# First attention of an eight-layer model: TensorE's order in a quartet written as a table of single steps

## The chip, the core and the metric

The kernel runs on one core of one Trainium2 chip. Its time is the device time of one execution in microseconds (us); the median of three runs before the change is 2110.02 (2104.93 to 2113.53). Everything is float32. A core has five engines that work side by side and wait for one another through semaphores: TensorE (PE in the profile; PEld is its weight load), VectorE (DVE), ScalarE (ACT), GpSimd (POOL) and SyncE (SP), which issues DMAs. Matmul results land in PSUM, which the kernel treats as eight banks of 128 x 512 numbers.

## The reference

The input x has shape (2, 512, 512): two batches (b) of 512 tokens with 512 features. Four attentions and four feed-forward layers follow, each of the form x = x + f(layernorm(x)). Only the first attention is changed:

```python
C_q  = x @ Wq_d  + bq_d                      # 512 -> 12
C_kv = x @ Wkv_d + bkv_d                     # 512 -> 4, keys and values share it
q = (C_q @ W_qk + b_qk).reshape(b, s, 32, 4)
scores = einsum('bqhd,bkd->bhqk', q, C_kv) / sqrt(4)
attn = softmax(scores)                       # no mask
V = (C_kv @ Wv_u + bv_u).reshape(b, s, 32, 16)
out = einsum('bhqk,bkhd->bqhd', attn, V).reshape(b, s, 512)
return out @ Wo + bo
```

There are 32 heads in each batch, with a contraction of only four numbers in the scores. The layer after it is a linear map with a low-rank adapter.

## The kernel before

`attn_latent_small` (from L416) does the first attention. A **quartet** is four heads of one batch: there are 16 quartets, 0 to 7 for batch 0 and 8 to 15 for batch 1. Head g of a quartet lies on partitions 32g to 32g+31 (`rows[g]`), so its matmuls use one of four row groups of the array, and four matmuls of different g can run at the same time. Each matmul is recorded as two passes of TensorE.

One quartet u consists of these steps, as functions:

- `score(u, qt, g)` (L560): for one head and one tile of 128 queries, TensorE computes the scores (L563) into a bank, and VectorE takes the row maximum (L571) into `nm[u % 2]`. There are 16 per quartet.
- `maxima(u)` (L575): four transposes of `nm` (L579), and VectorE adds the negated maxima to the queries, giving `qm` (L581).
- `transposed(u, kc, g)` (L584): TensorE computes the scores again with keys on the partitions and the maximum already subtracted (L598), and ScalarE takes the exponent into SBUF (L601). There are 16 per quartet.
- `values(u)` (L603): 16 matmuls that contract over all 128 partitions, four of them accumulating side by side into one bank (L609). ScalarE copies the result (L619) for the first quartet of a half batch, VectorE adds it to `raw` for the others (L621).

Every step takes its PSUM bank from `k.turn()`, which hands out the eight banks strictly in order, so a step can only begin once the step eight before it has been read out of its bank by VectorE or ScalarE.

After quartets 3, 7, 11 and 15 `divide` transposes `raw` and divides by the sums (L631, L636, L639). After quartets 7 and 15 `flatten` (POOL, L652) and `project` (L662, L664, L667) finish a batch and add it to x. `norms` starts the loads of the adapter layer (class `AdaptedBlock`, L729) after quartet 7, and normalises the tokens of batch 0 for it.

Some work runs between the quartets as **extra pieces**: for batch 1, four layernorms (transposes at L195), the latents and queries (chains of four matmuls, L162), two groups of head queries (L478) and the transposed values (L492); and, for the projection, `fold` and `fold_bias` (L501 to L525), which multiply Wv_u into Wo. There are eleven. `fold_bias` also adds a bias to all eight tiles of x on POOL.

`run_quartets` sets TensorE's order; the other engines' order is left to the scheduler, apart from `issue_after`. It first issues all 16 scores of quartet 0 and its maxima. Then, for each u, it alternates four scores of quartet u+1 with four exponents of quartet u, four times over; after each such round comes one extra piece, if any is left, or one of `after` (divide, flatten, project, norms) of an earlier quartet. Then come values(u) and maxima(u+1). In the last quartet the pieces of `ending` (the adapter's weights, its first products, the end of the attention) stand between the exponents. `run_ordered`, which the last attention uses, is another such function, with an order given as a string.

Of the kernel before, what the change touches and what calls it, by code (L numbers as in the profile page):

```python
# [37 lines left out]
B, S, D = 2, 512, 512  # L38
P = 128
NT = S // P  # L40
# [5 lines left out]
class Block:  # L46
# [292 lines left out]
                )  # L339

    @staticmethod
    def run_quartets(n, score, maxima, transposed, values, after, extra, ending):

        due, extra = [], list(extra)
        for u in range(-1, n - 1):
            pieces = [due.pop(0)] if due else []  # L350
            for j in range(NT):
                for m, (kind, g) in enumerate(
                    ((0, 0), (1, 1), (0, 2), (1, 3), (0, 1), (1, 0), (0, 3), (1, 2))
                    if j
                    else ((0, 0), (0, 1), (0, 2), (0, 3), (1, 0), (1, 1), (1, 2), (1, 3))
                ):
                    if kind == 0 and u + 1 < n:
                        score(u + 1, j, g)
                    if kind == 1 and 0 <= u < n:
                        transposed(u, j, g)  # L360
                if extra and u >= 0:
                    extra.pop(0)()
                elif pieces and j < 3:
                    of, done = pieces[0]
                    if done < len(after):
                        after[done](of)
                        pieces[0] = (of, done + 1)
            for of, done in pieces:
                for f in after[done:]:
                    f(of)  # L370
            if 0 <= u < n - 2:
                values(u)
                due.append((u, 0))
            maxima(u + 1)
        for i in range(NT * 4):
            transposed(n - 1, i // 4, i % 4)
            if i == 5:
                values(n - 2)
                for f in after:
                    f(n - 2)  # L380
            if i > 5 and i % 2:
                ending.pop(0)()
        ending.pop(0)()
        values(n - 1)
        for f in ending:
            f()

    @staticmethod
    def run_ordered(n, lead, order, score, maxima, transposed, values, after):

        scores = iter([(u, j, g) for u in range(n) for j in range(NT) for g in (0, 2, 1, 3)])
        for i in range(lead):
            score(*next(scores))
        for u in range(-1, n):
            left = [(j, g) for j in range(NT) for g in (1, 3, 0, 2)] if u >= 0 else []
            for step in order:  # L400
                if step == "S":
                    at = next(scores, None)
                    if at:
                        score(*at)
                elif step == "T" and left:
                    transposed(u, *left.pop(0))
                elif step == "M" and u + 1 < n:
                    maxima(u + 1)
                elif step == "|" and u > 0:
                    after(u - 1)  # L410
            if u >= 0:
                values(u)
        after(n - 1)


def attn_latent_small(k, a):  # L416
# [8 lines left out]
    with ExitStack() as ctx:  # L425
# [19 lines left out]
        for i in range(2):  # L445
            m = one([P, NT, P], f"nm{i}")
# [11 lines left out]
        def prepare(b):  # L458

            xT = k.xT[b]  # L460
            cq = one([P, S], "cq")

            def latents():
                ps = k.turn()
                k.chain(ps, [(wkvd[:, c], xT[:, c]) for c in range(KC)])
                nc.vector.tensor_scalar(keys[b], ps, bkvc, None, ALU.add)

            def queries():
                ps = k.turn()
                k.chain(ps, [(wqd[:, c], xT[:, c]) for c in range(KC)])  # L470
                nc.vector.tensor_scalar(cq, ps, bqd, None, ALU.add)

            def heads(half):
                for g in range(4):
                    t = 4 * half + g
                    own_rows = slice(32 * g, 32 * g + 32)
                    ps = k.turn()
                    nc.tensor.matmul(ps, wqk[own_rows, half], cq[own_rows], start=True, stop=True)  # L478
                    if b == 0 and g % 2:
                        nc.vector.tensor_scalar(  # L480
                            qs[b][:, t], ps, bqk[:, t : t + 1], 0.5, ALU.add, ALU.mult
                        )
                    else:
                        nc.scalar.activation(
                            qs[b][:, t], ps, AF.Identity, bias=halves[:, t : t + 1], scale=0.5
                        )

            def values():

                tp = k.turn()  # L490
                for t in range(NT):
                    nc.tensor.transpose(tp[:, bass.ts(t, P)], keys[b][:, bass.ts(t, P)], k.ident)  # L492
                part = tp.rearrange("p (t d) -> p t d", t=NT)[:, :, 0:5]
                for i in range(4):
                    to = vals[b][:, :, i, 5 * i : 5 * i + 5]
                    k.latest = nc.vector.tensor_copy(to, part).ins

            norms = [lambda t=t: k.layernorm(b * NT + t, k.turn) for t in range(NT)]
            return (norms if b else []) + [latents, queries, lambda: heads(0), lambda: heads(1), values]
# [45 lines left out]
        def behind(piece):  # L545

            def f():
                with tc.issue_after(first):
                    piece()
            return f  # L550

        with tc.issue_after(k.latest):
            adapter_coefficients(k, a)
        extra = [behind(f) for f in prepare(1) + [fold, fold_bias]]

        quartets = [(b, half, i) for b in range(B) for half in range(2) for i in range(4)]
        qm, probs, sums, ctxs = {}, {}, {}, {}
# [2 lines left out]
        def score(u, qt, g):  # L560
            b, half, i = quartets[u]
            ps = k.turn()
            nc.tensor.matmul(  # L563
                ps,
                qs[b][rows[g], 4 * half + i, bass.ts(qt, P)],
                keys[b][rows[g]],
                start=True,
                stop=True,
            )
            at = 32 * g + spare  # L570
            nc.vector.tensor_reduce(  # L571
                nm[u % 2][:, qt, at : at + 1], ps, AX.X, ALU.max, negate=True
            )

        def maxima(u):  # L575
            b, half, i = quartets[u]
            tp = k.turn()
            for qt in range(NT):
                nc.tensor.transpose(tp[:, bass.ts(qt, P)], nm[u % 2][:, qt], k.ident)  # L579
            t = lp.tile([P, S], F32, tag="qm", name="qm")  # L580
            nc.vector.tensor_tensor(t, tp, qs[b][:, 4 * half + i], ALU.add)  # L581
            qm[u] = t
# [20 lines left out]
        def values(u):  # L603
            b, half, i = quartets[u]
            acc = k.turn()
            for kc in range(NT):
                pt = probs.pop((u, kc))
                for g in range(4):
                    nc.tensor.matmul(  # L609
                        acc[rows[g]],  # L610
                        vals[b][:, kc, i],
                        pt[:, g],
                        start=(kc == 0),
                        stop=(kc == NT - 1),
                    )

            if i == 0:
                sums[b, half] = one([P, S], "raw")
                nc.scalar.copy(sums[b, half], acc)  # L619
            else:  # L620
                nc.vector.tensor_tensor(sums[b, half], acc, sums[b, half], ALU.add)  # L621
# [64 lines left out]
        last = len(quartets) - 1  # L686
        adapt = [lambda m=m: blocks[0].adapt(m) for m in range(KC)]
        feed = [lambda t=t: blocks[0].product(0, t) for t in range(NT)]

        tokens = [lambda t=t: k.layernorm(t, k.turn, back=True) for t in range(NT)]  # L690
        ending = [lambda: None] + adapt + feed[:2]
        ending += [lambda: divide(last), feed[2], lambda: flatten(last), feed[3]]
        ending += [lambda: project(last)] + tokens
        after = [divide, flatten, project, norms]
        with tc.manual_schedule(engines={mybir.EngineType.PE}):
            k.run_quartets(
                len(quartets), score, maxima, transposed, values, after, extra, ending
            )
        return blocks[0]


# [1159 lines left out]
```

## Time and profile before

| | us |
|---|---|
| three runs: median (lowest, highest) | 2110.02 (2104.93, 2113.53) |
| the profiled execution | 2103.46 |
| its span, first to last instruction | 2101.4 |
| first score of the first attention (L563) | 23.49 |
| first exponent matmul (L598) | 37.79 |
| maxima of quartets 6 and 7 (L579) | 139.93, 154.00 |
| values of quartets 14 and 15 (L609) | 276.55, 292.24 |
| mean granted clock of TensorE | 0.992 |

The profile is one execution. Times are microseconds from the start of the span. A row of a timeline gives the start, the length, the engine, the line, the operation, the output and the inputs by the program's names (so a bank is called sc, pj, tp or av), the shape and a count; in brackets stands how long the engine was idle before it, and what released it. A row of the table of waits gives the engine and its line, what it waited for, the total, how often and the longest. The stretches give, for each window, the busy time and count of PE, PEld, DVE, ACT and POOL, the granted clock of TensorE and the DMA share and rate.

### The profile page before, as it was taken

Reading aid. Unit: us, or ns where it says so; the run is one execution under the profiler, and the core shown is the slowest. Engines: PE = TensorE matmul, PEld = TensorE weight load, DVE = VectorE, ACT = ScalarE, POOL = GpSimd, SP = SyncE. Lnnn points to the kernel's source line nnn. Section 1 sums busy time; section 2 is a strip of 40 time slices with the busy share of each in tenths; the row PEclk is TensorE's granted clock in tenths of the full one; section 3 lists DMA queues with packets and bytes.
Section 4 is the critical chain, followed back from the end, with each engine's and each line's share of the span. In section 5 each row is a group of like instructions: output and inputs, shape, how many; then the busy total and the mean of one; then the engine's idle time right before and its main releaser. Section 6 shows DMA issues by size and latency. Waiting matters only on the chain. (4 is left out here: it accounts for less than half of the span.)

```text
span 2101.4 us, 40138 instructions
## 1 busy us (share of the span) xinstructions
PE 2031.9 (97%) x15560; PEld 1147.1 (55%) x15560; DVE 1351.0 (64%) x3575; ACT 745.4 (35%) x2072; POOL 970.4 (46%) x1239
## 2 busy tenths in 40 slices
PE   9999999999999999999999989999999999999998
PEld 5444435666666566666665544545454454654654
DVE  7678766756566566666664557666666784855845
ACT  3555632222222222222222145444544411441531
POOL 1101016776555557566653246555555555115220
PEclk9999999999999999999999999999999999999999
DMA  3001012222222222222220321010101003002001
GB/s 100 16 21 41 1 66 76 72 76 71 91 71 71 91 71 76 71 91 76 73 77 26 117 61 54 22 51 25 50 22 52 2 6 70 2 2 41 2 2 40
DMA packets 70221, 107.43 MB, mean 51 GB/s; under 512 B 13699, under 2 KB 50691, under 8 KB 63237
## 3 DMA queue, kind: packets, MB, share of 16 engines
q1 hardware_dynamic: 69380, 103.71, 15.6%
q8 instruction: 126, 2.06, 0.4%
q10 hardware_dynamic: 640, 1.05, 0.3%
q14 instruction: 75, 0.61, 0.1%
HBM read 80.61 MB, written 2.10 MB: 39 GB/s over the span
## 5 line engine op out<-in xcount | busy, mean ns | idle before, releaser
L263 ACT ACTIVATE room<-room,nmax 128x128 f32<-128x128 f32 (+3 forms) x384 | 212.3, 555 | 484.2 <-DVE nmax L253 482.7
L274 POOL TENSOR_SCALAR room<-room,invs 128x128 f32<-128x128 f32 (+3 forms) x384 | 198.0, 537 | 142.1 <-DVE invs L271 142.1
L314 PE MATMUL sc<-turned,vals 32*128 32x128 f32 (+7 forms) x1034 | 186.2, 411 | 1.3 <-DVE turned L287 1.3
L314 PE MATMUL pj<-turned,vals 32*128 32x384 f32 (+7 forms) x708 | 184.9, 422 | 0.0
L210 POOL TENSOR_TENSOR rstd<-ve,mhalf 128x1 f32<-128x1 f32 x80 | 45.9, 577 | 246.0 <-DVE ve L208 240.2
L314 PE MATMUL tp<-turned,vals 32*128 32x256 f32 (+7 forms) x770 | 147.1, 420 | 2.5 <-DMA vals<-v 2.1
L242 PE MATMUL sc<-kT,q 128*32 128x256 f32 (+4 forms) x1528 | 134.0, 384 | 6.8 <-DVE invs L271 4.1
L287 DVE STREAM_TRANSPOSE turned<-room 128x1152 f32<-128x1152 f32 x80 | 109.1, 1363 | 42.4 <-POOL room L274 39.9
L314 PEld LDWEIGHTS sc<-turned,vals 32*128 32x128 f32 (+1 forms) x1034 | 119.3, 166 | 14.3 <-issue 4.2
L943 POOL TENSOR_TENSOR q<-q,cosq 128x512 f32<-128x512 f32 x60 | 89.5, 1491 | 59.9 <-DVE t L940 59.9
L162 PE MATMUL sc<-w,room 128*128 128x512 f32 (+1 forms) x256 | 112.1, 582 | 0.0
L314 PEld LDWEIGHTS pj<-turned,vals 32*128 32x128 f32 (+1 forms) x708 | 104.0, 169 | 4.0 <-issue 1.6
L314 PEld LDWEIGHTS tp<-turned,vals 32*128 32x128 f32 (+1 forms) x770 | 97.6, 169 | 10.8 <-issue 4.9
L162 PE MATMUL sc<-w,ctxT 128*128 128x512 f32 x224 | 101.5, 596 | 0.0
L218 DVE TENSOR_TENSOR x<-sc,x 128x512 f32<-128x512 f32 x79 | 54.2, 686 | 73.0 <-PE sc L162 70.3
L242 PE MATMUL tp<-kT,q 128*32 128x512 f32 (+4 forms) x984 | 91.7, 407 | 4.5 <-DVE invs L271 3.8
L274 POOL TENSOR_SCALAR probs<-probs,invs 128x128 f32<-128x128 f32 (+3 forms) x128 | 65.8, 535 | 65.0 <-DVE invs L271 61.2
L263 ACT ACTIVATE probs<-probs,nmax 128x128 f32<-128x128 f32 (+3 forms) x128 | 71.1, 556 | 65.5 <-DVE nmax L253 64.3
L253 DVE CUSTOM_DVE_ANT_0 room<-sc,mask 128x256 f32<-128x256 f32 (+3 forms) x149 | 70.7, 474 | 35.6 <-PE sc L242 34.1
L242 PE MATMUL pj<-kT,q 128*32 128x288 f32 (+3 forms) x968 | 89.6, 404 | 2.9 <-POOL q L1211 1.9
L944 POOL TENSOR_TENSOR q<-q,t 128x512 f32<-128x512 f32 x64 | 88.0, 1374 | 6.5 <-DVE q L943 2.5
L1208 POOL TENSOR_TENSOR t<-t,sinq 128x512 f32<-128x512 f32 x32 | 40.8, 1276 | 106.4 <-DVE invs L271 100.6
(621 smaller groups left out, 6232.9 us busy)
## 6 DMA issues: line engine op xcount, KB each, us to landing
w<-in_b_wq SPq DMA_DIRECT2D x16, 1024.0 KB, 4.9
w<-in_b_wo SPq DMA_DIRECT2D x16, 1024.0 KB, 5.2
vals<-v SPq DMA_DIRECT2D x256, 64.0 KB, 2.0
w<-in_m_wo SPq DMA_DIRECT2D x8, 1024.0 KB, 7.2
w<-in_b_wk SPq DMA_DIRECT2D x16, 256.0 KB, 2.5
w<-in_b_wupv SPq DMA_DIRECT2D x16, 256.0 KB, 2.5
w<-in_f_w SPq DMA_DIRECT2D x4, 1024.0 KB, 6.0
w<-in_m_wqn SPq DMA_DIRECT2D x8, 384.0 KB, 3.1
```

Of the source, the lines that this page charges most:

```text
L162: last = self.nc.tensor.matmul(out, lhsT, rhs, start=(i == 0), stop=(i == len(pairs) - 1))
L210: self.nc.gpsimd.tensor_tensor(r, ve, self.mhalf, ALU.pow)
L218: self.latest = self.nc.vector.tensor_tensor(self.x[t], ps, self.x[t], ALU.add).ins
L242: nc.tensor.matmul(ps[32 * i : 32 * i + 32, a - lo : b - lo], q[:, at : at + 32], keys[:, a:b], start=True, stop=True,)
L253: nc.vector.tensor_tensor_reduce(out=row, in0=ps[:, :kv], in1=self.mask_back[:, :kv] if qt % 2 else self.mask[:, S - kv :], op0=ALU.add, o ...
L263: nc.scalar.activation(row, row, AF.Exp, bias=nmax, scale=-1.0, accum_out=total[:, qt : qt + 1])
L274: self.nc.gpsimd.tensor_scalar(row, row, inv[:, qt : qt + 1], 1.0, ALU.mult, ALU.mult)
L287: self.nc.vector.transpose(out[:, :last], probs[:, :last])
L314: self.nc.tensor.matmul(out[:, :, :n], values(i, j), rhs, start=(j == blocks[0]), stop=(j == stop[i]),)
L943: mul.tensor_tensor(q, q, tables["cosq"], ALU.mult)
L944: nc.gpsimd.tensor_tensor(q, q, t2, ALU.add)
L1208: nc.gpsimd.tensor_tensor(t2, t2, sinq, ALU.mult)
```

## The change

TensorE's order in the quartets is now a table of single steps, `order`, read by a new function `in_order`. `S10+2` is the score of tile 1 and head 0 for the quartet two ahead, `T32+0` the exponent step of key tile 3 and head 2 of the present quartet, `M` the maxima, `V` the values, and `|` a place for a piece. One reading of the table is one quartet. Twelve of a quartet's 16 scores are issued two or three quartets ahead. The maxima of the next quartet stand among the scores before the values, no longer behind them.

The reading starts three quartets early, so that three, then 12, then 16 scores precede the first exponents. In the last two of these readings an extra piece stands at each of the four bars, and in quartets 0, 1 and 2 one piece each at the second bar. `fold` and `fold_bias` are moved in the list, to stand ahead of and behind the queries. `divide`, `flatten`, `project` and `norms` come at the next bars after their quartet. In quartet 15 the list `ending` has lost its empty first entry, so that two of the adapter's products, and not one, stand ahead of the last values, and the divide follows the values directly.

```diff
+    @staticmethod
+    def in_order(n, order, do):
+        steps = [(s[0], int(s[1]), int(s[2]), int(s[3:])) if s != "|" else s for s in order.split()]
+        for p in range(-3, n + 3):
+            for step in steps:
+                if step == "|":
+                    if p > -3:
+                        do(p, step)
+                elif 0 <= p + step[3] < n:
+                    do(p + step[3], *step[:3])
...
-        extra = [behind(f) for f in prepare(1) + [fold, fold_bias]]
+        extra = [behind(f) for f in prepare(1)]
+        extra.insert(5, behind(fold))
+        extra.insert(7, behind(fold_bias))
...
-        ending = [lambda: None] + adapt + feed[:2]
+        ending = adapt + feed[:2]
...
-        after = [divide, flatten, project, norms]
+        def following(u):
+            b, half, i = quartets[u]
+            if i < 3:
+                return [norms] if b else []
+            return [divide, flatten, project, norms] if half else [divide]
+
+        order = (
+            "T32+0 S10+2 T23+0 S21+2 T30+0 S32+1 | T11+0 S03+2 T00+0 S22+1 T01+0 T03+0 "
+            "S00+1 S01+2 | T02+0 T33+0 S11+1 T20+0 T13+0 S12+2 T10+0 | T31+0 S23+2 T12+0 "
+            "M00+1 S30+3 S33+2 T21+0 | T22+0 S20+3 S13+2 S31+3 S02+2 V00+0 "
+        )
+        due, count = [], dict(pieces=0)
+
+        def do(u, kind, *at):
+            if kind == "|":
+                i = count["pieces"] = (count["pieces"] + 1) % 4
+                if extra and (u < 0 or i == 2):
+                    extra.pop(0)()
+                elif due:
+                    due.pop(0)()
+            elif kind == "S":
+                score(u, *at)
+            elif kind == "M":
+                maxima(u)
+            elif kind == "V" and u != last - 1:
+                if u == last:
+                    ending.pop(0)()
+                values(u)
+                if u < last:
+                    due.extend(lambda f=f: f(u) for f in following(u))
+            elif kind == "T":
+                if u == last:
+                    i = count["last"] = count.get("last", -1) + 1
+                    transposed(u, i // 4, i % 4)
+                    if i == 5:
+                        values(u - 1)
+                    elif i > 5 and i % 2:
+                        ending.pop(0)()
+                else:
+                    transposed(u, *at)
+
         with tc.manual_schedule(engines={mybir.EngineType.PE}):
-            k.run_quartets(
-                len(quartets), score, maxima, transposed, values, after, extra, ending
-            )
+            k.in_order(len(quartets), order, do)
+            for piece in ending:
+                piece()
```

More of the change, by code (lines that the diff above doesn't have):

```diff
@@ L341, in run_quartets @@
     @staticmethod
[L342 to L388, printed above, removed]
     def run_ordered(n, lead, order, score, maxima, transposed, values, after):
```

## The prediction

> **What bounds the stage.** I read, in this order: the page, the stage cut into stretches, the waits, then the timelines of TensorE and VectorE over one plain quartet. The page puts TensorE at 97% of the span, but a matmul counts as busy whether it uses one row group of the array or four, so that share settles nothing here.
>
> ```profile
> PE 2031.9 (97%) x15560; PEld 1147.1 (55%) x15560; DVE 1351.0 (64%) x3575; ACT 745.4 (35%) x2072; POOL 970.4 (46%) x1239
> ```
>
> The maxima's transposes (L579) mark a quartet's start: 31.89 (done only at 35.5), 53.28, 76.31, 97.19, 111.25, 125.87, 139.93, 154.00, 168.06, 187.22, 203.78, 218.87, 232.93, 247.55, 261.61, 272.11. A quartet without pieces takes 14.06 (139.93 to 154.00). Timeline of VectorE at the end of such a quartet (start, length, instruction, idle before it and its releaser), then TensorE's:
>
> ```profile
> 150.43 1.06 PE L609 MATMUL pj<-room,vals 128*32 128x512 f32 x8
> 154.00 0.44 PE L579 MATMUL tp<-ident,nm 128*128 128x128 f32 x2
> ```
> ```profile
> 151.02 0.68 DVE L571 TENSOR_REDUCE nm<-tp 128x1 f32<-128x512 f32 x1
> 154.13 0.69 DVE L621 TENSOR_TENSOR raw<-pj,raw 128x512 f32<-128x512 f32 x1 [2.43 <-PE pj L609]
> 154.76 0.69 DVE L581 TENSOR_TENSOR qm<-tp,qs 128x512 f32<-128x512 f32 x1
> 155.74 0.69 DVE L571 TENSOR_REDUCE nm<-sc 128x1 f32<-128x512 f32 x1 [0.29 <-PE pj L563]
> ```
>
> Reduces start 0.60 apart when queued, so VectorE has 18 x 0.60 = 10.8 per quartet (16 reduces, raw, qm). It then idles 2.43 while TensorE does the values (3.57) and has no score to hand over, and 0.29 until the next scores. While VectorE runs, TensorE waits for banks:
>
> ```profile
> PEld sc L563 <- DVE nm L571: 11.3, 36, 0.7
> PEld tp L563 <- DVE nm L571: 8.6, 26, 0.7
> PEld pj L563 <- DVE nm L571: 7.3, 23, 0.6
> ```
>
> So the two engines alternate: VectorE sets the pace in the scores, TensorE in the values. TensorE's own need is 8 groups of four concurrent score/exponent matmuls at 0.96 (140.52 to 141.48) = 7.7, values 3.57, transposes 0.59: 11.9. ScalarE needs 16 x 0.49 = 7.8.
>
> **The plain quartet.** The table keeps every instruction and only reorders them. Four scores stand right before the values, so VectorE has up to 4 x 0.6 = 2.4 of queued work in those 3.57; with the roughly 0.3 until fresh scores after the values, about 1.5 of idleness remains. Another stage of this trace already queues scores ahead of its values; its idle gap is the nearest row:
>
> ```profile
> 1816.10 0.46 DVE L1585 CUSTOM_DVE_ANT_0 sc<-sc,mask 128x256 f32<-128x256 f32 x1
> 1816.48 0.14 DVE L1585 DVE_READ_ACCUMULATOR2_ANT nm<- 128x1 f32 x1
> 1818.07 0.57 DVE L1585 CUSTOM_DVE_ANT_0 sc<-sc,mask 128x384 f32<-128x384 f32 x1 [1.45 <-PE sc L1575]
> ```
>
> The maxima's transposes now stand between scores, six steps behind the last score they need. qm is added long before the eight steps and the values that precede its use, so today's wait for qm (0.61 to 0.65 before L598) goes. What would be late next is the reduce before the transposes: queued behind the transposes are all later scores, for which VectorE waits. At that point two more scores (1.2 of VectorE work) plus qm (0.6) are queued; the transposes (0.59) plus the first new score's way to VectorE (1.16: first pass 140.52, reduce 141.68) make 1.75. It just closes.
>
> A rule speaks against the table: the Trainium skill, "TensorEngine Tiling (Array Packing)", Key Properties, says a change of tiling mode drains the array. Per quartet the modes changed three times (scores to values to transposes to scores), now four. The row: a pass that follows a mode change starts 0.52 after the one before (149.91 to 150.43), against 0.43 between passes of one mode, so a switch costs 0.1, and the groups of four are complete at both cuts. If the drain had to be paid in full, each extra cut would cost a pass, 0.43, and 14 quartets 6 us rather than 1.4. I take the row. Sum: 10.8 + 1.45 + 0.1 = 12.35, say **12.4**; bounds 11.4 (hole nearly covered; below TensorE's 11.9 because a group without waits needs 0.86) and 14.06 + 1.15 (rival C). Saved: 14.06 - 12.4 = 1.66 in each of quartets 0 to 13, 23.2.
>
> **The start.** Before, 16 scores run from 23.49 and the first exponents start at 37.79. Now 31 scores (3, 12 and 16) and eight of eleven pieces precede them. The first 15 scores are paced by VectorE: first reduce 25.23, 15 x 0.6 = 9, adapter and xn operations 1.6, so 35.8; TensorE is some four scores ahead, 33.5, with the four transpose pieces (0.66 each) in the shadow. Then each of the four chains takes 3.5:
>
> ```profile
> 55.79 3.70 PE L162 MATMUL pj<-room,w 128*128 128x512 f32 x8
> 61.39 3.70 PE L162 MATMUL tp<-room,w 128*128 128x512 f32 x8
> ```
>
> 4 x 3.5 = 14.0, 16 scores in five groups 4.8, transposes 0.6, ten switches 1.0: 20.4; VectorE's 16 x 0.6 plus four evacuations lie beside it. The clock comes on top. Stretches of the start (time, TensorE busy and count, other engines, granted clock):
>
> ```profile
> 28.00:32.00 4.00, 4.00 (x13) 1.58 (x12) 4.00 (x9) 0.00 (x0) 0.00 (x0) 0.95 0.00 0
> 32.00:36.00 4.00, 1.53 (x8) 0.61 (x8) 3.46 (x6) 0.00 (x0) 0.00 (x0) 0.50 0.00 0
> 36.00:40.00 4.00, 4.00 (x18) 1.49 (x19) 2.66 (x5) 0.26 (x1) 0.00 (x0) 0.50 0.00 0
> 40.00:44.00 4.00, 4.00 (x27) 2.05 (x25) 2.64 (x5) 3.82 (x9) 0.00 (x0) 0.77 0.00 0
> ```
>
> One score per 0.6 lets the clock fall to half, and it comes back about 5 us after dense work resumes at 35.9. The Trainium skill, "TensorE: Matmul & The Clock Gate", Part 1, has the clock fall only after an idle window of some 3.4 us; by that rule the transpose pieces between the scores keep it up and nothing is lost. The row shows the fall while TensorE still counts as busy, so I charge 2.5 (5 us at half speed; bounds 0 and 5). First exponents: 33.5 + 20.4 + 2.5 = 56.4, which is 18.6 later. In return quartets 0 to 2 lose the pieces: before, 37.79 to 98.74 (97.19 + 0.59 + 0.96) is 60.95, less 3 x 14.06, so 18.8 of pieces; left are two head pieces (1.0 each) and one transpose piece (0.8): 16.0 back. Net **-2.6**. The bias additions on POOL (9.89 from 92.57) move up with them; they are next needed by the projection in quartet 8. No DMA moves past another: the loads behind the adapter's (184.81, 187.39) stay in quartet 8, whose other extra (20.6 against 14.06) I carry over whole.
>
> **The end.** Quartet 14 keeps only four scores and quartet 15 none. Before, values of 14 start at 276.55, 13.4 after its first exponents (263.16). Now ScalarE sets it: 16 x 0.49 + 1.2 + about 0.9 for banks, 9.9: **+3.5**. Beside this the last values' divide loses the product that stood between; its transposes must wait for raw, 0.69 plus two hand-overs: **-0.9**.
>
> ```profile
> 295.81 3.70 PE L162 MATMUL sc<-adapted,room 128*128 128x512 f32 x8
> 299.34 0.60 PE L631 MATMUL pj<-ident,raw 128*128 128x128 f32 x4
> ```
>
> **Sum.** 23.2 - 2.6 + 3.5 - 0.9 = 23.2 gained; the other terms cancel, so the gain is 14 x (14.06 - quartet). Profiled execution: 2103.46 (span 2101.4 and 2.1 around it) becomes 2080.3. That execution lies 6.6 below the median of the three runs, 2110.02, so for the median I forecast **2087**, range of this case 2078 to 2096. The attention that follows starts behind this stage's last projection, and its weights are requested when this stage frees their buffers, so both move together.
>
> **Rivals.**
> A, chance 0.17: scores keep VectorE fed through the values, and TensorE packs at 0.86: quartet 11.4, gain 37, **2073**. For it: 0.43 passes occur back to back (144.75, 145.18). Against: banks are handed out in order from eight, so a queue of waiting scores stops TensorE.
> B, chance 0.22: that ring eats the lead. A bank is held 1.16 + 0.69 even with no queue, and with three scores waiting 3.7, which allows 0.46 per step against 0.24 needed; the hole only halves, quartet 13.4, gain 9, **2101**, half of it within 0.5%.
> C, chance 0.16, slower: VectorE's order is not the table's, and if the reduce that the maxima need comes late, TensorE stands at the transposes with its scores behind it and VectorE runs dry: 0.59 + 1.16 - 0.6 (qm) = 1.15 more per quartet, with the old hole at the values still there: 15.2, loss 16, **2126**. It decides from 14.8 per quartet on (loss 10.5). For it: TensorE already waited up to 1.24 and 0.79 for a reduce at L579 (189.01, 273.44). Against: both in quartets where other work crowded VectorE or the values came later.
> The case forecast keeps 0.45. Faster: 0.45 + 0.17 + half of B, less a little for the spread, 0.70; same 0.16; slower 0.14. A change of 0.5% (10.5) is about what runs that spread from 2104.93 to 2113.53 can tell. To leave out no more than 2 in 10 the range runs from 2068 (A with a warm start) to 2114 (B entire, most of C outside).
>
> **What would show it.** Right: quartets near 12.4 between L579's starts; VectorE idle near 1.5 before raw; qm followed by no wait at L598; first exponents (L598) near 56; the granted clock at half for some 5 us before; values of quartet 14 under 10 after its first exponents. Wrong: L579 waiting over 0.6 for nm in most quartets (C), or L563 still stopped by nm as often as now with quartets over 13 (B).

## The result and the profile after

The change makes the kernel faster by about half of what was forecast. The median goes from 2108.30 us (six runs, 2104.60 to 2113.53) to 2095.59 us (six runs, 2094.97 to 2098.67): a ratio of 0.9945, 95% interval 0.9930 to 0.9959. By that ratio the gain is 11.6 us, between 8.6 and 14.8 (the medians themselves lie 12.7 apart); a median of 2087 and a gain of 23.2 were forecast. The profiled execution went from 2103.46 to 2095.05, its span from 2101.4 to 2093.0, so 8.4 us less. At this stage's last projection matmul the two traces stand 9.8 apart (310.60 before, 300.78 after), at the first scores of the last attention 9.0 (1785.11 and 1776.12). In between the granted clock falls in different places: in the changed kernel's trace it is 0.83 from 386 to 396 us and 1.00 in the same work before, and 1.7 of the 9.8 are gone behind that. The edit does not touch that work, so the steps below are counted to the stage's last projection.

The first part of the page says as little as it did before; TensorE counts as busy for 97% of the span:

```profile
PE 2028.5 (97%) x15560; PEld 1152.4 (55%) x15560; DVE 1354.0 (65%) x3575; ACT 741.2 (35%) x2072; POOL 969.1 (46%) x1239
```

The maxima's transposes (now L549) come at 48.14, 64.84, 80.30, 94.52, 107.44, 121.35, 134.21, 147.13, 160.06, 179.54, 195.25, 209.58, 222.50, 236.40, 249.32, 261.26. A plain quartet takes **12.92**; it took 14.06, and 12.4 was forecast. Timeline of TensorE after the change, the cuts of the plain quartet (maxima, first values, first exponent matmul behind them):

```profile
147.13 0.66 PE L549 MATMUL sc<-ident,nm 128*128 128x128 f32 x4
149.65 1.06 PE L579 MATMUL pj<-room,vals 128*32 128x512 f32 x8
153.22 0.69 PE L568 MATMUL tp<-qm,keys 32*128 32x512 f32 x1
```

The timeline of VectorE over the same quartet, after the change (in brackets its idle time and what ended it):

```profile
140.50 0.69 DVE L591 TENSOR_TENSOR raw<-tp,raw 128x512 f32<-128x512 f32 x1 [0.87 <-PE tp L579]
141.50 0.69 DVE L541 TENSOR_REDUCE nm<-pj 128x1 f32<-128x512 f32 x1 [0.30 <-PE sc L533]
...
145.09 1.87 DVE L541 TENSOR_REDUCE nm<-sc 128x1 f32<-128x512 f32 x3
147.03 0.69 DVE L541 TENSOR_REDUCE nm<-pj 128x1 f32<-128x512 f32 x1
147.83 0.69 DVE L551 TENSOR_TENSOR qm<-sc,qs 128x512 f32<-128x512 f32 x1
148.88 0.69 DVE L541 TENSOR_REDUCE nm<-pj 128x1 f32<-128x512 f32 x1 [0.36 <-PE av L568]
...
151.88 0.68 DVE L541 TENSOR_REDUCE nm<-sc 128x1 f32<-128x512 f32 x1
153.36 0.69 DVE L591 TENSOR_TENSOR raw<-pj,raw 128x512 f32<-128x512 f32 x1 [0.80 <-PE pj L579]
```

From raw to raw 12.86 pass. Eighteen instructions at 0.60 are 10.8; the rest, read from the starts, is 0.88 before raw and 0.40 behind it (the hole at the values, 1.28), and 0.79 around the maxima: 0.14 before the last reduce, 0.20 before qm and 0.45 behind it. The nine reduces behind raw follow each other 0.60 apart.

The prediction rests on no timeline of ScalarE. Here it is, first of the kernel before, then of the changed one:

```profile
142.70 0.60 ACT L601 ACTIVATE room<-sc 128x512 f32<-128x512 f32 x1 [5.60 <-PE sc L598]
...
150.57 0.60 ACT L601 ACTIVATE room<-sc 128x512 f32<-128x512 f32 x1
```
```profile
141.51 0.60 ACT L571 ACTIVATE room<-sc 128x512 f32<-128x512 f32 x1 [4.39 <-PE sc L533]
...
147.72 0.75 ACT L571 ACTIVATE pt<-tp 128x512 f32<-128x512 f32 x1
148.96 0.60 ACT L571 ACTIVATE pt<-sc 128x512 f32<-128x512 f32 x1 [0.48 <-PE av L568]
149.46 0.59 ACT L571 ACTIVATE pt<-av 128x512 f32<-128x512 f32 x1
154.44 0.60 ACT L571 ACTIVATE pt<-tp 128x512 f32<-128x512 f32 x1 [4.39 <-PE sc L533]
```

Before, ScalarE stood for 5.60, and sixteen exponents took 8.47 (142.70 to 151.17): together 14.07. Now fourteen of them follow each other 0.48 apart without a break (141.51 to 148.47, 6.96), two more come by 150.05, and the hole is 4.39: together 12.93. The sixteen exponents take no less (8.54 from the first to the last); on this engine the 1.14 of a quartet is the smaller hole.

The waits of the first stage, 23.4 to 300 us, after the change (engine and line, waited for: total, times, longest). Before, the table had 96 waits of scores for a reduce (31.1 us) and 14 waits of scores or exponent matmuls for an exponent (5.0 us). Now it has 6 and 60 (2.2 and 18.2 us): what stops TensorE is a bank that ScalarE still holds.

```profile
PEld pj L568 <- ACT pt L571: 2.3, 5, 0.7
...
PEld sc L568 <- ACT pt L571: 1.9, 5, 0.8
...
PEld sc L533 <- ACT pt L571: 1.7, 8, 0.4
...
PEld pj L533 <- DVE nm L541: 1.3, 3, 0.8
```

(Exponent matmuls also show waits of 0.8 for a reduce, 17 of them. Of these, 13 stand right behind the values, where the wait of 0.84 covers the switch described further down; they are not counted here.)

At the start the granted clock did not fall (columns as in the prediction's stretches):

```profile
28.00:32.00 4.00, 4.00 (x17) 1.80 (x16) 4.00 (x8) 1.17 (x2) 0.00 (x0) 1.00 0.00 0
32.00:36.00 4.00, 4.00 (x21) 1.83 (x20) 3.61 (x7) 0.59 (x1) 0.00 (x0) 1.00 0.00 0
36.00:40.00 4.00, 4.00 (x16) 1.45 (x15) 3.47 (x6) 0.00 (x0) 0.00 (x0) 1.00 0.23 66
```

At the end, TensorE's timeline shows the wait that was forecast for the divide:

```profile
289.46 0.66 PE L601 MATMUL pj<-ident,raw 128*128 128x128 f32 x4 [0.89 <-DVE raw L591]
```

### The profile page after: what moved, and what is told of

It is laid out like the page before. It is cut to its first block, busy times and chain, and to the rows that moved or that the text cites. A ratio compares the mean times of both kernels' runs of the same rounds, so it can differ in the third digit from the quotient of the medians.

```text
span 2093.0 us, 40127 instructions
## 1 busy us (share of the span) xinstructions
PE 2028.5 (97%) x15560; PEld 1152.4 (55%) x15560; DVE 1354.0 (65%) x3575; ACT 741.2 (35%) x2072; POOL 969.1 (46%) x1239
## 5 line engine op out<-in xcount | busy, mean ns | idle before, releaser
L568 PE MATMUL sc<-qm,keys 32*128 32x512 f32 x206 | 96.8, 628 | 0.0
```

What stands on the lines that cost most here:

```text
L568: nc.tensor.matmul(ps, keys[b][rows[g], bass.ts(kc, P)], qm[u][rows[g]], start=True, stop=True)
```

## The experiments

Three questions stood open: what sets the 12.92, where the gain in a quartet comes from, and what the start really costs. On the first, theory 1 said that ScalarE paces the stretch between the values and the maxima, because the table puts 14 of 16 exponents there; theory 2, the prediction's own, that VectorE's queue does. Line numbers of edits are those of the changed kernel.

| run | quartet | last projection matmul of the stage at | time |
|---|---|---|---|
| kernel before | 14.06 | 310.60 | 2108.30 |
| the change | 12.92 | 300.78 | 2095.59 |
| half_max_after | 12.92 | 301.93 | 2099.50 |
| half_exp_after | 12.77 | 296.5 | 2095.37 |
| half_both | 11.87 | 286.83 | 2083.00 |
| half_max_before | 13.38 | 294.8 | 2092.04 |
| maxima_behind | 14.34 | 318.58 | 2113.82 |
| more_scores | 13.35 | 309.81 | 2104.76 |
| pieces_as_before | 12.92 | 308.35 | 2107.47 |
| heads_front | 12.92 | 296.89 | 2094.42 |
| front_all | 12.92 | 296.97 | 2091.92 |

The half runs and maxima_behind are single executions; for those the quartet is the reading. The kernel before, run again beside the later runs, had medians of 2104.78 to 2107.51.

The last column mixes in something that none of these edits touches. In the traces of heads_front, half_exp_after and pieces_as_before the granted clock falls to half for 17 us, from 1214, 1212 and 1226 us on; in the changed kernel's it is 1.00 from 1204 to 1244 us. The same two passes, first in heads_front, then after the change:

```profile
1220.76 2.07 PE L1202 MATMUL sc<-lat,q_pe 128*128 128x512 f32 x2 [0.27 <-ACT kT L1152]
```
```profile
1223.42 1.13 PE L1203 MATMUL sc<-lat,q_pe 128*128 128x512 f32 x2 [0.21 <-ACT kT L1153]
```

heads_front, 3.89 ahead of the changed kernel at the stage's last projection, is 1.51 behind it at the last attention's first scores. The third column is therefore the one to compare; why the clock falls there in some executions and not in others, no run shows.

**Half the reduces.** Each reduce reads half of its score, so half of the maximum is left out; nothing else changes.

```diff
-                nm[u % 2][:, qt, at : at + 1], ps, AX.X, ALU.max, negate=True
+                nm[u % 2][:, qt, at : at + 1], ps[:, : S // 2], AX.X, ALU.max, negate=True
```

> The changed kernel, but each row maximum of the first attention is taken over half of the 512 scores (half of the maximum is left out), so a VectorE reduce should take about 0.33 in place of 0.60. Theory 1: in the 24 steps between the values and the maxima ScalarE paces too (14 exponents, one every 0.48, 6.7 in all, without a gap in the trace), so a plain quartet stays at 12.6 to 12.9. Theory 2 (the prediction's): VectorE alone paces and its holes are what is left, so the quartet falls to TensorE's own 12.0 or less.

Measured: 12.92, to the hundredth. ScalarE's timeline of this run is the changed kernel's, shifted:

```profile
142.32 0.60 ACT L571 ACTIVATE room<-sc 128x512 f32<-128x512 f32 x1 [4.39 <-PE sc L533]
...
148.55 0.74 ACT L571 ACTIVATE pt<-tp 128x512 f32<-128x512 f32 x1
```

A reduce was 0.42 long there and not 0.68, so VectorE was given some 4 us per quartet and the quartet took none of it. Theory 2 falls in the form it had: VectorE's queue alone is not the pace. The fourteen exponents stand 0.48 apart as before, and by themselves hold the quartet at 12.92.

**Half the exponents.** Each exponent makes half of its tile and the values read that half twice, so half of the exponents is left out.

```diff
-            nc.scalar.activation(probs[u, kc][:, g], ps, AF.Exp)
+            nc.scalar.activation(probs[u, kc][:, g, : S // 2], ps[:, : S // 2], AF.Exp)
...
-                        acc[rows[g]],
+                        acc[rows[g]].rearrange("p (n s) -> p n s", n=2),
                         vals[b][:, kc, i],
-                        pt[:, g],
+                        pt[:, g, : S // 2].unsqueeze(1).broadcast_to([P, 2, S // 2]),
```

> The changed kernel, but ScalarE takes only half of each exponent tile and the values read that half twice (half of the exponents is left out, TensorE's work is the same), so an exponent takes about 0.27 in place of 0.48. Theory 1: ScalarE stops holding banks, VectorE still needs 6.6 in the first 24 steps, so a plain quartet falls a little, from 12.9 to about 12.5. Theory 2: ScalarE has no part in it, the quartet stays at 12.9.

Measured: 12.77, between the two theories. ScalarE now has gaps in about half of the places between its exponents, but the quartet loses only 0.15, so theory 1 alone isn't the whole of it either. VectorE's timeline of this run has the reduces closed up, the hole at the values, and idle time around the maxima:

```profile
133.17 0.68 DVE L551 TENSOR_TENSOR qm<-pj,qs 128x512 f32<-128x512 f32 x1
134.17 0.69 DVE L541 TENSOR_REDUCE nm<-tp 128x1 f32<-128x512 f32 x1 [0.32 <-PE tp L568]
...
137.17 0.68 DVE L541 TENSOR_REDUCE nm<-pj 128x1 f32<-128x512 f32 x1
138.67 0.69 DVE L591 TENSOR_TENSOR raw<-tp,raw 128x512 f32<-128x512 f32 x1 [0.81 <-PE tp L579]
139.80 0.69 DVE L541 TENSOR_REDUCE nm<-pj 128x1 f32<-128x512 f32 x1 [0.44 <-PE sc L533]
```

Read like the changed kernel's: 10.8 for eighteen instructions, 1.43 for the hole at the values, 0.54 around the maxima (0.14 before the last reduce, 0.40 behind qm), together 12.77. That is what VectorE needs when ScalarE is out of the way.

**Both halves.** The two edits together.

> The changed kernel with both halvings: each row maximum over half of the scores, and half of each exponent tile, read twice by the values (half of the maximum and half of the exponents left out). The theory after the two single ones (12.92 and 12.77 against 12.92): in the 24 steps before the maxima ScalarE (14 x 0.48 = 6.7) and VectorE (raw and ten reduces, 6.6) are level, so only both together let the quartet fall, to TensorE's own 11.8 to 12.1. Rival: TensorE's order in the row groups is the pace, quartet 12.6 to 12.8.

Measured: 11.87, from the maxima in TensorE's timeline:

```profile
128.08 0.66 PE L549 MATMUL pj<-ident,nm 128*128 128x128 f32 x4
...
139.94 0.66 PE L549 MATMUL sc<-ident,nm 128*128 128x128 f32 x4
```

So the two engines pace that stretch almost level. From the values to the maxima VectorE has raw and ten reduces, 11 x 0.60 = 6.6, ScalarE fourteen exponents, 14 x 0.48 = 6.7. To relieve one leaves the other. The quartet with both, 12.92, is the longer of the two limits (12.92 with the reduces halved, 12.77 with the exponents halved), not more than either. With both relieved it falls to about TensorE's own need, which the prediction had put at 11.9.

**Half the reduces in the kernel before.** The same edit at its L571.

> The kernel before, with each row maximum over half of the scores (half of the maximum is left out). The prediction's reading of the kernel before, VectorE sets the pace between the values: a plain quartet falls from 14.06 to about 13 (TensorE 12.0 plus the 0.6 wait for qm, which stays). Rival, the ring of banks and ScalarE set it: stays above 13.7.

Measured: 13.38, between the two expectations. VectorE, which the prediction named as the pace of the scores, held the old quartet for 0.68 only; behind it came ScalarE, whose sixteen exponents then followed each other 0.48 apart, with a hole of 5.48 to 5.44 left.

**The maxima behind the values.** The table is kept, but `M` is moved to its front, as in the kernel before; the scores that were three quartets ahead become two ahead, which the move asks for.

```diff
-            "T32+0 S10+2 T23+0 S21+2 T30+0 S32+1 | T11+0 S03+2 T00+0 S22+1 T01+0 T03+0 "
+            "M00+0 S10+2 S21+2 S32+1 S03+2 T32+0 T23+0 T30+0 | T11+0 T00+0 S22+1 T01+0 T03+0 "
...
-            "M00+1 S30+3 S33+2 T21+0 | T22+0 S20+3 S13+2 S31+3 S02+2 V00+0 "
+            "S30+2 S33+2 T21+0 | T22+0 S20+2 S13+2 S31+2 S02+2 V00+0 "
```

> The changed kernel with the maxima moved back behind the values and followed by four scores, as before the change; the scores that stood three quartets ahead stand two ahead. Theory: what the table brings are the scores queued in front of the values, so a plain quartet stays at 12.7 to 13.1. Rival: the gain is the wait for qm that went (0.61 to 0.65), so the quartet is 13.5 or more.

Measured: 14.34, slower than the kernel before; the theory of this expectation was wrong and its rival right. ScalarE's timeline, then VectorE's, of this run:

```profile
148.78 0.60 ACT L571 ACTIVATE room<-pj 128x512 f32<-128x512 f32 x1 [6.46 <-PE av L568]
```
```profile
146.22 0.69 DVE L591 TENSOR_TENSOR raw<-sc,raw 128x512 f32<-128x512 f32 x1 [2.16 <-PE sc L579]
```

ScalarE's sixteen exponents are dense here too, and their 7.9 and a hole of 6.46 make the quartet. So the scores issued ahead and their interleaving gain nothing while the maxima stand behind the values. With the maxima ahead of them qm is ready before the values, and exponents can follow the values at once. This edit moves more than the maxima, though: four scores go behind them and three exponents later. And the opposite case, the old order with the maxima alone moved ahead, was not run.

**One more score before the values.** One score and one exponent step change places, so that five scores stand there.

```diff
-            "... T20+0 T13+0 S12+2 T10+0 ... | T22+0 S20+3 ..."
+            "... T20+0 T13+0 T22+0 T10+0 ... | S12+2 S20+3 ..."
```

> The changed kernel with one more score (S12) in the run in front of the values and one exponent (T22) in its old place: 15 exponents in the first 24 steps. Theory 1 (ScalarE paces those steps): they take 0.45 longer while VectorE's hole at the values, 0.80 to 0.87, shrinks to about 0.3; quartet 12.8 to 13.0, time within 3 of the changed kernel. Theory 2 (VectorE alone): the hole's 0.5 is gained, quartet 12.4, time 6 to 7 lower, 2089.

Measured: 13.35, longer than either theory allowed; the time is 2104.76, ratio to the kernel before 0.9984 (0.9975 to 0.9993). The fifteenth exponent in the stretch costs 0.43, close to its 0.48 on ScalarE, and the longer queue for VectorE gives nothing back. Theory 1 was right in what paces the stretch, and wrong to set VectorE's smaller hole against it.

**The pieces where they were.** The table is kept, but `fold` and `fold_bias` stand at the end of the list again, and pieces come at every bar from quartet 0 on.

```diff
-        extra.insert(5, behind(fold))
-        extra.insert(7, behind(fold_bias))
+        extra += [behind(fold), behind(fold_bias)]
...
-                if extra and (u < 0 or i == 2):
+                if extra and u >= 0:
```

> The changed kernel with all eleven pieces back in quartets 0 to 2, four in each, in their old order; the table and the 31 scores in front stay. Theory: without the transposes between the first scores the granted clock falls to half again for 5 to 10 us, the first exponents come near 45, and quartets 0 to 2 take 18.8 of pieces and about 3 of ScalarE waits more, so quartet 3 begins at 103 to 106 (100.6 in the changed kernel); time 3 to 5 above the changed kernel, 2098 to 2101. Rival: where the pieces stand makes no difference, quartet 3 within 1 of 100.6 and the time near 2095.6.

Measured: 2107.47 against 2107.51 of the kernel before beside it, a ratio of 0.9992 (0.9983 to 1.0001), though the plain quartets are 12.92. The first exponents come at 42.15, and quartet 3's at 108.2, later than was expected: 66.0, less 3 x 12.92, is 27 for pieces that cost 18.8 in the old quartets. At the stage's last projection this run is 2.25 ahead of the kernel before and 7.6 behind the changed one, and the clock's fall near 1226 us costs it about 5 more. So the table without the new places of the pieces keeps less than a quarter of the 9.8. The stretches of this run also show the clock at the start:

```profile
28.00:32.00 4.00, 4.00 (x14) 2.31 (x14) 4.00 (x8) 0.00 (x0) 0.00 (x0) 0.88 0.00 0
32.00:36.00 4.00, 4.00 (x15) 2.76 (x15) 4.00 (x8) 0.00 (x0) 0.00 (x0) 0.50 0.00 0
36.00:40.00 4.00, 2.95 (x11) 1.01 (x7) 4.00 (x8) 0.00 (x0) 0.00 (x0) 0.50 0.00 0
```

The scores are paced by VectorE as in the changed kernel; the transposes between them are gone, and the clock is at half from 32 to 44 us.

**The head queries in front, the rest inside.** Here `fold` and `fold_bias` come last, so that they fall into quartets 0 and 1 and the head queries ahead of the first exponents; `ending` gets its empty first entry back.

```diff
-        extra.insert(5, behind(fold))
-        extra.insert(7, behind(fold_bias))
+        extra[8:8] = [behind(fold), behind(fold_bias)]
...
-        ending = adapt + feed[:2]
+        ending = [lambda: None] + adapt + feed[:2]
```

> The changed kernel with the two groups of head queries in front of the first quartet and fold and fold_bias behind them, in quartets 0 and 1; and with the empty first entry back in the list of the end. Theory: the head queries' four evacuations on ScalarE (0.59 each) are what made quartets 0 and 1 3.7 and 2.5 longer than a plain one where 1.0 each was counted; in front ScalarE is idle. First exponents near 48.5, quartets 0 and 1 near 16.5 (a chain of 3.5 each), quartet 3 begins near 96 in place of 100.6. At the end the divide waits no longer for raw, 0.9 less. Time 2090 to 2091. Rival: the chains stop VectorE as long as the head queries stop TensorE, quartet 3 begins within 1 of 100.6, time 2095.

Measured: first exponents 49.28, quartets 0 and 1 are 17.9 and 17.3 with a chain each, quartet 3's exponents at 98.7 (100.61 in the changed kernel): 1.9 gained, where some 4.6 were expected. A chain of full-array matmuls, 3.5 long, costs 4.4 to 5.0 where it stands in a quartet. The time is 2094.42, ratio 0.9923 (0.9897 to 0.9948), from four runs: 2091.45 and 2092.07 with a mean granted clock of 0.992, 2096.76 and 2096.92 with 0.988, and the trace, of the last, has the fall at 1214 us. The entry at the end can be told apart: the last projection is 3.89 earlier than in the changed kernel, the values of 14 only 1.93, so 1.96 comes from the end.

**Everything in front.** Both chains and both head queries precede the first exponents; only the values' transposes stay in quartet 0; `ending` as in the run above.

```diff
-        extra.insert(5, behind(fold))
+        extra.insert(4, behind(fold))
...
-        ending = adapt + feed[:2]
+        ending = [lambda: None] + adapt + feed[:2]
...
+                    if u == -2 and i in (1, 2):
+                        extra.pop(0)()
```

> The changed kernel with all pieces but the transposed values in front of the first exponents: two layernorms at each of the first two bars, then fold and latents, then queries, fold_bias and the two groups of head queries; values (its four transposes) in quartet 0; and the empty first entry back in the list of the end. Theory: a chain inside a quartet cost 4.4 to 5.0 for 3.5 of matmuls (quartets 0 and 1 of the kernel with the heads in front: 17.9 and 17.3), while the first 15 scores are paced by VectorE and leave TensorE free. First exponents near 54 (49.3 there), quartet 0 near 14, quartets 1 and 2 at 12.9, quartet 3 begins near 94 (98.7 there, 100.6 in the changed kernel); time 2089 to 2090. Rival: VectorE runs dry during the two chains just as inside a quartet; first exponents at 57 or later, quartet 3 at 97 or later, time 2093 or more.

Measured: the first exponents come at 58.17 and quartet 3's at 98.77, as in the run before; both lie where the rival had them. Between them lie 40.6, the three plain quartets and 1.8, which quartet 0 takes more with the values' transposes in it. The two chains, moved from quartets 0 and 1 to the front, put the first exponents back by 8.89, 4.4 each, about what they cost inside. But here the first one ran partly at half clock. TensorE had stood for 0.99 ahead of a layernorm piece, the granted clock fell (0.85 from 28 to 32 us, 0.72 from 32 to 36), and the chain took 5.14 where the others take 3.70, with VectorE out of work behind it. Timelines of TensorE and VectorE, and the stretches of this run:

```profile
29.00 0.66 PE L195 MATMUL sc<-ident,xn 128*128 128x128 f32 x4 [0.99 <-DVE xn L182]
...
31.31 5.14 PE L162 MATMUL pj<-w,wv_diag 128*128 128x512 f32 x8
```
```profile
36.48 0.43 DVE L487 COPY wv_diag<-a_bvu 128x512 f32<-128x512 f32 x1 [4.37 <-PE pj L162]
```
```profile
28.00:32.00 4.00, 3.01 (x12) 1.63 (x12) 3.18 (x6) 1.07 (x2) 0.00 (x0) 0.85 0.00 0
32.00:36.00 4.00, 4.00 (x8) 1.54 (x6) 0.11 (x1) 0.00 (x0) 0.00 (x0) 0.72 0.00 0
```

Without that, 1.44, the two would have cost 7.45 at the front, 3.7 each (an estimate from these lengths), so a place in front may be the cheaper one. The median is the lowest of the kernels that leave nothing out: 2091.92 (2089.68 to 2095.22), ratio 0.9929 (0.9914 to 0.9945). At the stage's last projection it is level with heads_front (296.97 and 296.89), whose two runs at a clock of 0.992 lie in the same range. Beside it on the same chip the unaltered change ran once more:

> The changed kernel itself, unaltered, on the same chip as the one with all pieces in front, to compare the two: 2095 to 2097, plain quartets 12.92, quartet 3 begins at 100.6.

Measured: 2095.73 (2095.39 to 2097.29), ratio 0.9946 (0.9932 to 0.9959), the first measurement again. The intervals of the two ratios overlap, but no run of one lies among those of the other. The 3.81 between the medians has its place in the traces: 1.85 at the start (values of 14 at 262.92 rather than 264.77) and 1.96 at the end.

## Why the prediction was half right

The sum by its own steps, each read at the traces' marks, to the stage's last projection:

| step | forecast | measured |
|---|---|---|
| 14 plain quartets | +23.2 | +16.0 (14 x 1.14) |
| start, to quartet 3's exponents without the quartets | -2.6 | -5.3 |
| extra of quartet 8, of 9 to 13, and the divide in 3 to 7 | 0 | -2.9 (-1.4, -1.1, -0.4) |
| exponents of 14 to its values | +3.5 | +4.0 |
| values of 14 to the last projection | -0.9 | -2.0 |
| sum | +23.2 | +9.8 |

**The plain quartet: the step that failed.** The mechanism was right: four scores queued before the values keep VectorE at work through most of them. Its hole there is 1.28, where 1.45 was put down. Two other terms were wrong.

The first is the step at the maxima, "It just closes", with 0.1 for a switch. VectorE idles 0.79 there. The way from the maxima's transposes to the next reduce is the 1.75 that was forecast (147.13 to 148.88). The work queued for VectorE at that point was forecast as two scores and qm, 1.8. The rows show one score and qm, 1.2: the last reduce but one had started at 146.29 and its 0.60 were over before the transposes began. The drain rule that the prediction cites asked for no more than its row gave: 0.52 from pass to pass at the switch (146.61 to 147.13).

The second is "ScalarE needs 16 x 0.49 = 7.8", by which ScalarE was no limit. It is an average over a quartet; the table puts fourteen of the sixteen exponents between the values and the maxima, 6.7 in one piece, level with VectorE's 6.6 there. The half runs part the two. With ScalarE relieved VectorE's own sum is 12.77, so 0.4 of the 0.5 to 12.92 is the first error. With VectorE relieved ScalarE holds the quartet at 12.92, so a VectorE sum of 12.4 would not have brought 12.4 either. Each error alone breaks the forecast; half_both shows that nothing else of that size stands behind them.

The wait for banks that ScalarE holds is the prediction's rival B in part: 12.92 lies between 12.4 and B's 13.4, and the time between its 2101 and 2087. But B's mark, scores stopped by reduces as often as before, isn't there: 6 such waits, not 96.

**The maxima's place.** For TensorE it closes as argued. The last reduce that the maxima of 147.13 need is the one that starts at 145.69, two before the last, so it is done at 146.37, while the last exponent pass ahead of the maxima starts only at 146.61; the maxima follow that by 0.52, the price of a switch. (TensorE's weight loads do stand 0.76 at L549, with a reduce named in 11 of the 16 quartets, which by the prediction's mark of 0.6 would mean rival C. They stand as long ahead of the values, and stood 0.84 at the maxima of 139.93 before, with nothing named: it is the time around a switch, and the mark was badly chosen.) For qm only one wait of scores, 1.0 in quartet 8, is left, and none of exponents. Rival C, where VectorE's order makes the maxima late, did not come. The prediction counted this step as the loss of a wait of 0.65. maxima_behind suggests that it is worth more, since with the maxima behind the values the scores issued ahead give 14.34; what the move is worth alone stays open.

**The start.** Two errors of opposite sign. The clock stayed at 1.00, so the 2.5 charged for it was not lost and the first exponents came at 54.39, not 56.4. The Trainium skill, "TensorE: Matmul & The Clock Gate", Part 1, has the clock fall only after some 3.4 us of idleness, and the prediction had drawn from it that the transposes between the scores keep it up. That came true: none of the eight traces with one such piece at each bar has a fall at the start, and pieces_as_before, without them, fell to 0.50 in the same scores. The reason is not shown. In pieces_as_before a score ran every 0.6 us and TensorE counted as busy while the clock fell, so idleness as the profile counts it is not what decides. The row of before (0.50 at one score per 0.6) was of scores alone; it did not cover the case. The second error is larger. For the pieces left in quartets 0 to 2 the sum had 2.8; from 54.39 to 100.61 it is 46.22, less 3 x 12.92, so 7.46. By quartets 3.7, 2.5 and 1.3 for the two head pieces and the transposes, where 1.0, 1.0 and 0.8 were put down. A head piece isn't only its matmuls: as the rows read, its evacuations on ScalarE stand between the exponents, TensorE waits for them, and VectorE runs dry. Timelines of ScalarE, of TensorE's loads and of VectorE in quartet 0 of the changed kernel:

```profile
62.08 0.69 ACT L452 ACTIVATE qs<-sc,halves 128x512 f32<-128x512 f32 x1
```
```profile
62.81 0.29 PEld L568 LDWEIGHTS sc<-qm,keys 32*128 32x128 f32 x2 [0.28 <-ACT qs L452]
```
```profile
62.16 0.69 DVE L541 TENSOR_REDUCE nm<-pj 128x1 f32<-128x512 f32 x1 [0.92 <-PE sc L568]
64.46 0.69 DVE L541 TENSOR_REDUCE nm<-av 128x1 f32<-128x512 f32 x1 [0.75 <-PE av L533]
```

It reads as the second error again, ScalarE taken for free where its exponents were dense; no run tests it alone. With both head pieces moved to the front (front_all) quartets 0 to 2 are 5.6 shorter and the first exponents 3.8 later, 1.4 of that for the clock.

**What was carried over.** The extra of quartet 8 was taken over "whole"; it grew from 6.5 to 7.94, that of quartets 9 to 13 from 2.66 to 3.8, and the divides' from 0.57 to 0.93. That the plain quartet has less slack, so that what is put in costs more of its length, would explain it and fits pieces_as_before (27 for 18.8), but was not tested.

**The end.** Values of 14 came 9.37 after its first exponents; 9.9 was forecast, and ScalarE sets it as said. The divide's wait is the forecast one, 0.89. Not seen was that with the empty entry gone every piece of the adapter stands one place earlier too, so that four exponents that ran as one group become two groups of two: from the end of 14's values to the first product the changed kernel takes 9.52, heads_front, where they are back, 8.48. Together about 1.96, which heads_front and front_all got back.

**The clock outside the stage.** The profiled spans lie 8.4 apart, the medians 12.7. The two profiled executions have the same mean granted clock, 0.992. All twelve runs of the changed kernel lie at 0.991 to 0.993. Of the 39 runs of the kernel before that stood beside heads_front, one lies at 0.992, and it took 2103.29; the others lie at 0.984 to 0.990 and take up to 2113.68. At an equal clock, then, the change is worth about 8, a third of the 23.2, and the rest of the measured gain goes with the clock. Where it fell in those runs of the kernel before is not recorded; in the three traces above it was in a stage that the edits do not touch. That the result came out at half of the forecast owes that much to luck, or to an effect of the change on the later clock; no run tells which.

## What to carry to other kernels

Where one engine feeds two others through a ring of buffers, add up each engine's work for each stretch between two fixed points, not for the whole loop; an engine that is busy for half of the loop can still be the pace of the half into which its work was moved. Look at the timeline of every engine on the loop before calling one free, and price a piece in a tightened loop anew, since the slack that hid it may be what the tightening took. Put the producer of a value that the next round waits for ahead of a long block, here the maxima ahead of the values: without that the fine interleaving around it was worth nothing. And compare runs at a mark behind the stage that was changed, with the granted clock beside it, before reading the total time.

## What the runs showed of the hardware

- The granted clock follows something other than the busy column: from 28 to 36 us TensorE counted 4.00 of 4.00 in both, but in pieces_as_before scores of 32 rows at VectorE's pace ran the clock down to 0.50, and in the changed kernel the same scores with groups of four transposes of 0.66 among them kept it at 1.00.
- The clock can also fall in one execution of the same work and not in another: in heads_front to 0.50 for about 17 us from 1214 us on, where two passes then took 2.07 and not 1.13. It cost that run about 5 us.
- A full-array chain of 3.5 us costs 4.4 to 5.0 between matmuls of 32 rows in a quartet (heads_front).
- ScalarE's exponents of 128x512 start 0.48 apart when dense although each is shown 0.59 to 0.75 long, VectorE's reduces 0.60 apart at 0.68 (the changed kernel); a sum over the shown lengths would be too high by a quarter or more for the first and by an eighth for the second.
